# The last routing of a mixture-of-experts block: where the base table is built, in which order POOL lists and gathers, and which buffers the last products use

## The chip, the cores and the metric

The kernel runs on one core of one Trainium2 chip. TensorE (PE) multiplies and transposes, VectorE (DVE) and ScalarE (ACT) work elementwise, GpSimd (POOL) issues the indirect DMAs, SyncE (SP) issues the plain loads; ACT issues some plain DMAs too. The metric is device time in microseconds, lower is better.

## The reference, cut to what matters

There are 2048 tokens of 512 numbers, in float32. The first block is a layernorm, 16 heads of linear attention over 4 groups of keys, an output product with `Wo`, and the residual. The second block is a layernorm and a mixture of experts:

```python
scores = softmax(xf @ w_cls.T)                 # 64 logits: 32 experts, 32 that do nothing
_, topk_idx = top_k(scores + bias, 8)
w = take_along_axis(scores, topk_idx); w = w / (w.sum(-1) + EPS) * 1.5
# every expert takes its tokens in order, at most 256 of them
act = silu(x_e @ gate[e]) * (x_e @ up[e])      # 512 -> 256
y_e = act @ w_down[e]                          # 256 -> 512
out = (sum over a token's experts of w * y_e) * (1 + weights of the idle ones)
x = x + out
```

How many tokens an expert gets depends on the data, so the kernel finds at run time which rows each expert needs.

## The kernel before, in words

**The attention part.** Four blocks of 512 tokens run one after the other, each as four chunks of 128 tokens (16 chunks in all). `output` (L374 to L394) makes one chunk's output product `px` from 16 heads (L382; each shows as two matmuls in the trace), adds the residual into `x1` (L385), stores it (L386), takes mean and variance (L388, L390), lets POOL raise the variance to the power -1/2 (L263) and leaves the normalized chunk in `xw` (L393). A product of a chunk is 16 heads in order, and `between` lets other work in after the first 8.

**Routing.** `route` (L396 to L483) transposes `xw` (`prt`, L400), makes 64 logits (L405), finds the top 8 on DVE, writes the normalized row and its 32 weights to the array `rows` in HBM (L435), counts the position of each token within each expert, collects in `held` (L467) which token has which of the first 32 places of each expert, and leaves eight table addresses per token in `ai` (L482). `list_further` (L197) then issues eight indirect DMAs on POOL (`slots<-tok,ai`, L200). They write the token's number into eight tables in HBM. `place` has ranked the experts by their load of the first chunks, and places and tables go by that rank.

**Base and further places.** The first 32 places of each expert are the base. Four experts make one base group of 128 rows, so there are 8 groups. `rows_so_far` (L511 to L530) belongs to them: SP loads the tables' first 32 places (`idx_8b`, L516), DVE takes the lowest (`low`, L518; `low_f`, L520), PE transposes (`p_low`, L522), DVE spreads (`lowT`, L524), PE puts it in the experts' order (`p_place`, L526) and DVE reduces it to `idx_m_f` (L529, L530), the base table from the listings so far. It is called ahead of the product of the last chunk, chunk 15, and the routing of chunk 14 comes in the middle of that product. The last chunk's own part of the base comes from `held`; both meet in `idx_f` (L647 to L649) and `idx_b` (L650). The other places, 32 to 255, are read by ACT from the tables (`idx<-slots`, L835, eight loads), reduced by DVE (`idx_e`, L838), and put in order by PE and DVE (L840 to L847) into `idx`.

**The experts.** `gather` (L679) is an indirect DMA on POOL that fetches rows. `group_up` and `group_down` treat a base group: transposes (`pe_b`, L728), products (`pu_b`, L742), `act_b` (L746, L747), `aT_b` (L757), the down product, `y_b` (L762), a product that adds rows of the same token (`ps`, L764), `z` (L766) and a scatter-add of z into the output (L714). `over` treats one expert's further rows, 128 and 96: transposes (L728), `pu` (L786), `aT` (L789, L790), `py` (L801), a scaled `y` for the first part by ACT (L810) and for the second by DVE (L808), and a scatter-add of each (L714). The tiles `y` come from a pool of three buffers. The scatter-adds wait for one another one by one: y, y, z, y, y, z and so on. The first expert of each of the 8 groups always runs (two parts). The experts of rank 8 and up run in a nest of conditions, `further` (L868), which gathers ahead by three ranks (`xg_n`), and has a buffer `xg_r` for a second part. In the profiled run ranks 8, 9 and 10 ran, with one part each.

**Order.** Statements are put on the engines' queues by a planner that knows priorities and dependences; `issue_after` ties a statement's place to another's end in the queue. Each engine works its queue in order. Weights come in pairs of experts (`load_pair`, L185 and L194) on SP's queue, two of 1 MB and two of 0.5 MB a pair. The first three pairs are issued freely, and pair 3 waits for the second base gather (`behind`).

Of the kernel before, what the change touches and what calls it, by code (L numbers as in the profile page):

```python
# [9 lines left out]
F32 = mybir.dt.float32  # L10
# [3 lines left out]
ALU = mybir.AluOpType  # L14
# [4 lines left out]
P = 128  # L19
S = 2048  # L20
# [47 lines left out]
def linattn_moe(  # L68
# [125 lines left out]
            nc.sync.dma_start(out=dn[:, j], in_=wdn[bass.ds(v, 1)].rearrange("e (k p) f -> p (e k) f", p=P))  # L194
            weights[2 * i + j] = weights[2 * i + j], dn[:, j]

    def list_further(ch, ai):  # L197

        for k in range(TOPK):
            nc.gpsimd.indirect_dma_start(  # L200
                out=slots[k][:, :],
                out_offset=bass.IndirectOffsetOnAxis(ap=ai[:, k : k + 1], axis=0),
                in_=tok[:, ch : ch + 1],
                in_offset=None,
                bounds_check=NS - 1,
                oob_is_err=False,
            )


    with ExitStack() as ph:  # L210
# [163 lines left out]
        def output(sb, c, oTs, between=None):  # L374

            ch = sb * NC + c
            xs, _, _ = blocks[sb]
            px = p_pj.tile([P, D], F32, tag="pj", name=f"px_{ch}")
            for h in range(H):
                if between is not None and h == H // 2:  # L380
                    between()
                nc.tensor.matmul(px, lhsT=oTs[h // R][:, h % R, ts(c, P)], rhs=wo[h // R][:, h % R, :],  # L382
                                 start=(h == 0), stop=(h == H - 1))
            x1 = tmp.tile([P, D], F32, tag="row", name=f"x1_{ch}")
            nc.vector.tensor_tensor(x1, px, xs[:, c, :], ALU.add)  # L385
            tc.chain_iter_dep("out", nc.scalar.dma_start(out=out[ts(ch, P), :], in_=x1).ins)  # L386
            st = sml.tile([P, 6], F32, tag="st", name=f"st2_{ch}")
            nc.vector.bn_stats(st, x1)  # L388
            mv = sml.tile([P, 2], F32, tag="mv", name=f"mv2_{ch}")
            nc.vector.bn_aggr(mv, st)  # L390
            rstd = rstd_of(mv[:, 1:2], 1, f"2_{ch}")
            xw = tmp.tile([P, XW], F32, tag="xw", name=f"xw_{ch}")
            nc.vector.tensor_scalar(xw[:, :D], x1, mv[:, 0:1], rstd, ALU.subtract, ALU.mult)  # L393
            return xw  # L394
# [117 lines left out]
        def rows_so_far():  # L512

            idx_8b = tmp.tile([SL, TOPK, E], I32, tag="rb", name="idx_8b")
            for k in range(TOPK):
                nc.sync.dma_start(out=idx_8b[:, k, :], in_=slots_v[k][:SL, :E])  # L516
            low = sml.tile([SL, E], I32, tag="low", name="low", bufs=1)
            nc.vector.tensor_reduce(low, idx_8b.rearrange("s k e -> s e k"), AX.X, ALU.min)  # L518
            low_f = sml.tile([SL, E], F32, tag="hi", name="low_f")
            nc.vector.tensor_copy(low_f, low)  # L520
            pt = p_ms.tile([E, SL], F32, tag="ms", name="p_low")
            nc.tensor.transpose(pt, low_f, ident[:SL, :SL])  # L522
            lowT = sml.tile([E, Q, SL], F32, tag="fT", name="lowT", bufs=1)
            nc.vector.tensor_copy(lowT, pt.unsqueeze(1).to_broadcast([E, Q, SL]))  # L524
            pn = p_ms.tile([P, NQ, Q], F32, tag="ms", name="p_place")
            nc.tensor.matmul(pn, lhsT=lowT.rearrange("e j s -> e (j s)"), rhs=placed[:E, :E],  # L526
                             start=True, stop=True)
            part = sml.tile([P, NQ, Q], F32, tag="ad", name="part")
            nc.vector.tensor_tensor(part, pn, mine.unsqueeze(1).to_broadcast([P, NQ, Q]), ALU.mult)  # L529
            nc.vector.tensor_reduce(idx_m_f, part, AX.X, ALU.add)  # L530
# [15 lines left out]
        for sb in range(NSB):  # L546
            last = sb == NSB - 1
            if not last:
                blocks[sb + 1] = load_block(sb + 1)
            for g in range(G):  # L550
                if g == 0:
                    vas = [values(sb, c, xTs[sb]) for c in range(NC)]
                if g + 1 < G:
                    projs[sb, g + 1] = project(sb, g + 1, xTs[sb])
                elif not last:
                    xTs[sb + 1] = norm_block(sb + 1)
                    projs[sb + 1, 0] = project(sb + 1, 0, xTs[sb + 1])
                if last and g == 1:
                    rank_e = place()
                if last and g == G - 1:  # L560
                    for i in range(2):
                        load_pair(i)
                oT = otp.tile([P, R, SB], F32, tag="oT", name=f"oT_{sb}_{g}")
                oTs[sb, g] = oT
                for c in range(NC):
                    attend(sb, g, c, projs[sb, g], vas[c], oT)
                    if g == G - 1:
                        if c != 1 and waiting:
                            route_and_list(*waiting.pop(0))
                        if c >= 1:  # L570
                            waiting.append((sb * NC + c - 1,
                                            output(sb, c - 1, [oTs[sb, i] for i in range(G)])))
            listed = []
            if last:
                rows_so_far()
            xw = output(sb, NC - 1, [oTs[sb, i] for i in range(G)],
                        (lambda: listed.append(route(*waiting.pop(0)))) if last else None)
            with tc.issue_after(rstd_of.last.ins):
                for one in listed:
                    list_further(*one)  # L580
            while waiting:
                route_and_list(*waiting.pop(0))
            if last:
                route(sb * NC + NC - 1, xw)
            else:
                waiting.append((sb * NC + NC - 1, xw))
# [12 lines left out]
            nc.tensor.matmul(pn[:, i, :], lhsT=more_than[:, i : i + 1].to_broadcast([E, P]), rhs=of,  # L599
                             start=True, stop=True)  # L600
        big = sml.tile([P, 2, 2, E // 2], F32, tag="big", name="big")
        nc.vector.tensor_scalar(big.rearrange("p i a b -> p i (a b)"), pn, 0.5, None, ALU.is_ge)
        bigf = big.rearrange("p i a b -> p (i a) b")
        nc.vector.tensor_tensor(bigf, bigf, bits.unsqueeze(1).to_broadcast([P, 4, E // 2]), ALU.mult)
        bsum = sml.tile([P, 4], F32, tag="bsum", name="bsum")
# [11 lines left out]
    q_y = ctx.enter_context(tc.tile_pool(name="q_y", bufs=2, space=PSUM))  # L617
    NF = FI // P
    M2 = CAP - C2
    EARLY = 3  # L620
    FIRST = 2

    idx8 = xgp.tile([P, TOPK, 2 * E], I32, name="idx8")
# [15 lines left out]
    xg_b = [xgp.tile([P, XW], F32, name=f"xg_b{i}") for i in range(NQ)]  # L639
    xg_o = [xgp.tile([P, XW], F32, name=f"xg_o{i}") for i in range(2)]  # L640
    xg_t = [xgp.tile([P, XW], F32, name=f"xg_t{i}") for i in range(2)]
    xg_n = [xgp.tile([P, XW], F32, name=f"xg_n{i}") for i in range(3)]
    xg_r = xgp.tile([P, XW], F32, name="xg_r")
    for t in xg_o + xg_t + xg_n + [xg_r]:
        nc.scalar.mul(t, ident[:, 0:1].to_broadcast([P, XW]), 0.0)

    nc.vector.scalar_tensor_tensor(idx_f, held[:, :, 1], float(P), held[:, :, 0], ALU.mult, ALU.add)  # L647
    nc.vector.scalar_tensor_tensor(idx_f, idx_f, float(NONE), idx_m_f, ALU.add, ALU.min)
    nc.vector.tensor_tensor(idx_f, idx_f, nobody_f, ALU.min)  # L649
    nc.vector.tensor_copy(idx_b, idx_f)  # L650

    def find_same():

# [21 lines left out]
    def column(n, i):  # L675
        return idx[:, i * E + n : i * E + n + 1]

    def gather(t, i, n):
        return nc.gpsimd.indirect_dma_start(  # L679
            out=t,  # L680
            out_offset=None,
            in_=rows[:, :],
            in_offset=bass.IndirectOffsetOnAxis(ap=i, axis=0),
            bounds_check=n - 1,
            oob_is_err=False,
        )
# [85 lines left out]
    def over(e, parts, behind=None):  # L772
# [30 lines left out]
                at += k  # L803
        ys = []
        for i, (py, (xg, k)) in enumerate(zip(pys, parts)):
            y = yp.tile([P, D], F32, tag="y", name=f"y_{n}_{i}")
            if i:
                nc.vector.tensor_scalar(y[:k], py[:k], ws[i][:k], None, ALU.mult)  # L808
            else:
                nc.scalar.mul(y[:k], py[:k], ws[i][:k])  # L810
            ys.append((y[:k], column(e, i)[:k]))
# [5 lines left out]

    load_pair(2)
    base = []
    for q in range(EARLY):  # L820
        g = gather(xg_b[q], idx_b[:, q : q + 1], XR)
        base.append(g)
    for i in range(3, AHEAD_W):
        load_pair(i, base[1])
    with tc.issue_after(g.ins):
        list_further(S // P - 1, ai_last)
        for q in range(EARLY, NQ):
            gather(xg_b[q], idx_b[:, q : q + 1], XR)
    ahead = group_up(0)
# [19 lines left out]
    def gather_first(q):  # L849
        gather(xg_o[q % 2], column(Q * q, 0), S)  # L850
        return gather(xg_t[q % 2], column(Q * q, 1), S)

    def number_of(r):
        q, j = place_of(r)
        return Q * q + j

    def gather_rank(r):
        gather(xg_n[r % 3], column(number_of(r), 0), S)

    def reload(n, r):  # L860

# [8 lines left out]
    def further(r):  # L870

        n = number_of(r)
        with tc.If(more(0, r)):  # L873
            if n // Q < LATE:
                reload(n, r)
            with tc.If(more(1, r)) as cond:
                gather(xg_r, column(n, 1), S)
                over(n, [(xg_n[r % 3], P), (xg_r, M2)])
            with cond.Else():
                over(n, [(xg_n[r % 3], P)])  # L880
            if r + 3 < E:
                gather_rank(r + 3)
            if r + 1 < E:
                further(r + 1)

# [66 lines left out]
```

## Time and profile before

| what | value |
|---|---|
| median of the runs | 1140.47 us (three runs, 1138.63 to 1142.53) |
| the profiled execution | 1131.0 us, its span 1129.2 us, mean granted TensorE clock 0.964 |
| PE busy | 1025.8 us, 91% of the span |
| DVE, ACT, POOL busy | 607.5, 209.4, 229.8 us |
| scatter-adds into the output (L714) | 27, 19 of y and 8 of z, 2.6 / 5.8 / 8.5 us from issue to landing (min, median, max) |
| listing of the last chunk (`slots<-tok,ai_last`) | 8 DMAs, 2.6 / 5.1 / 6.3 us to landing |
| loads of the tables (`idx<-slots`) | 8 DMAs, 2.6 / 3.1 / 5.3 us to landing |
| base gathers (`xg_b<-rows,idx_b`) | 8 DMAs, median 3.8 us to landing |
| share of the 16 DMA engines in use | 0.38 at 880 to 900 us, 0.84 at 910 to 930, 1.02 at 950 to 1000, 0.26 at 1050 to 1080 |

A row of the timeline has the start in us, the duration in us, the engine (SPq, ACTq: a DMA issued by that engine's queue), the line, the operation, output and inputs by the program's names, shapes, and how many instructions were taken together; in brackets stands how long the engine had been idle and what ended that. A row of the waits has the waiting engine and line, what it waited for, and the total, the number and the longest of these waits. Figures after the share of the span are busy time; idle time of an engine that sets nothing costs nothing.

### The profile page before, as it was taken

What the parts mean: (1) busy time and instruction counts of PE and PEld (TensorE: products, weight loads), DVE (VectorE), ACT (ScalarE), POOL (GpSimd) and SP (SyncE); (2) the same over time, 40 slices, a digit from 0 to 9 for tenths busy, and PEclk for the clock granted to TensorE, in tenths of its full rate; (3) what the DMA queues carried; (4) which work ended last, traced back from release to release, by engine and by line L of the source; (5) the groups of instructions that cost most, each with busy time, mean ns of one, the idle gap of its engine ahead of it and who ended that gap; (6) DMA issues with size and microseconds to landing.
All of it is one profiled execution on the core that took longest, in us unless ns stands there. A gap on an engine that the chain in (4) does not pass through costs nothing. (4 is left out here: it accounts for less than half of the span.)

```text
span 1129.2 us, 12758 instructions
## 1 busy us (share of the span) xinstructions
PE 1025.8 (91%) x4420; PEld 581.3 (51%) x4420; DVE 607.5 (54%) x1661; ACT 209.4 (19%) x543; POOL 229.8 (20%) x290
## 2 busy tenths in 40 slices
PE   6999899999998999999899999999988677998883
PEld 3455455544655555455465544555643335675452
DVE  5778864347786733388847324778532532222220
ACT  1122221001233200122232001222200210111110
POOL 6000000431000044300001432000142364322332
PEclk9999999999999999999999999999999768999897
DMA  9400000010000000100000000023001379999220
GB/s 344 167 1 1 19 1 10 30 66 1 1 1 19 1 30 29 57 1 1 1 1 11 29 20 20 1 87 138 15 26 46 116 239 392 332 377 380 48 27 6
DMA packets 51805, 87.25 MB, mean 77 GB/s; under 512 B 11342, under 2 KB 11470, under 8 KB 51728
## 3 DMA queue, kind: packets, MB, share of 16 engines
q1 hardware_dynamic: 35248, 67.31, 16.2%
q0 software_dynamic: 10720, 10.08, 4.1%
q10 hardware_dynamic: 5760, 8.92, 2.1%
q8 instruction: 38, 0.62, 0.2%
q14 instruction: 39, 0.32, 0.1%
HBM read 75.92 MB, written 15.88 MB: 81 GB/s over the span
## 5 line engine op out<-in xcount | busy, mean ns | idle before, releaser
L382 PE MATMUL px<-wo,oT 128*128 128x512 f32 x512 | 234.7, 603 | 0.0
L324 PE MATMUL pq<-xT,wq 128*128 128x512 f32 x512 | 230.5, 595 | 0.5 <-DVE rb_q L306 0.4
L200 POOL DMA_INDIRECT slots<-tok,ai x120 | 117.7, 981 | 241.7 <-DVE ai L482 209.5
L324 PEld LDWEIGHTS pq<-xT,wq 128*128 128x128 f32 x512 | 93.5, 191 | 106.6 <-issue 91.7
L382 PEld LDWEIGHTS px<-wo,oT 128*128 128x128 f32 x512 | 94.5, 194 | 98.2 <-issue 98.1
L346 PE MATMUL po<-va,at 128*128 128x129 f32 x512 | 99.3, 280 | 12.1 <-DVE at L339 11.8
L355 ACT ACTIVATE osb<-po,den 128x128 f32<-128x128 f32 x256 | 77.7, 365 | 151.5 <-DVE den L353 85.6
L346 PEld LDWEIGHTS po<-va,at 128*128 128x128 f32 x512 | 80.0, 193 | 35.7 <-DVE at L339 23.3
L349 PE MATMUL po<-state,qT 128*128 128x129 f32 x480 | 93.6, 277 | 0.0
L295 POOL MEMSET va<- 128x4 f32 x16 | 1.5, 110 | 412.0 <-PE pst L362 412.0
L349 PEld LDWEIGHTS po<-state,qT 128*128 128x128 f32 x480 | 73.5, 193 | 1.3 <-DVE state L365 0.8
L371 PE MATMUL pot<-ident,osb 128*128 128x128 f32 x256 | 60.8, 302 | 14.5 <-ACT osb L355 13.3
L309 ACT ACTIVATE rb_q<-rb_q 128x512 f32<-128x512 f32 x64 | 40.3, 630 | 179.2 <-DVE rb_q L308 164.1
L385 DVE TENSOR_TENSOR x<-px,xs 128x512 f32<-128x512 f32 x16 | 11.1, 692 | 108.8 <-PE px L382 108.7
L371 PEld LDWEIGHTS pot<-ident,osb 128*128 128x128 f32 x256 | 36.1, 146 | 62.5 <-ACT osb L355 49.5
L337 PE MATMUL psc<-qT,kT 128*128 128x512 f32 x128 | 68.2, 616 | 0.0
L786 PE MATMUL pu<-xeT,gu 128*128 128x224 f32 (+1 forms) x352 | 63.8, 341 | 4.1 <-DVE xeT L729 4.1
L786 PEld LDWEIGHTS pu<-xeT,gu 128*128 128x128 f32 x352 | 60.3, 195 | 6.3 <-ACT y L810 2.3
L339 DVE TENSOR_TENSOR at<-psc,causal 128x512 f32<-128x512 f32 x64 | 44.0, 687 | 32.0 <-PE psc L337 31.9
L317 PE MATMUL pk<-xT,wk 128*128 128x512 f32 x128 | 58.9, 595 | 0.8 <-ACT xT L284 0.7
L372 DVE COPY oT<-pot 128x512 f32<-128x512 f32 x64 | 43.9, 686 | 25.8 <-PE pot L371 25.7
L292 PE MATMUL pv<-wv,xT 128*128 128x512 f32 x128 | 57.0, 596 | 0.0
(223 smaller groups left out, 1192.3 us busy)
## 6 DMA issues: line engine op xcount, KB each, us to landing
gu<-in_wgu_dram SPq DMA_DIRECT2D x32, 1024.0 KB, 12.0
dn<-in_wdn_dram SPq DMA_DIRECT2D x32, 512.0 KB, 12.4
rows<-xw ACTq DMA_DIRECT2D x16, 272.0 KB, 2.0
wq<-in_wqT_dram SPq DMA_DIRECT2D x4, 1024.0 KB, 14.8
wo<-in_woT_dram SPq DMA_DIRECT2D x4, 1024.0 KB, 14.6
out_dram<-x ACTq DMA_DIRECT2D x16, 256.0 KB, 2.1
xs<-in_x_dram SPq DMA_DIRECT2D x3, 1024.0 KB, 7.4
slots<-tok,ai POOLq DMA_INDIRECT x120, 2.1
```

The source lines that it names most:

```text
L200: nc.gpsimd.indirect_dma_start(out=slots[k][:, :], out_offset=bass.IndirectOffsetOnAxis(ap=ai[:, k : k + 1], axis=0), in_=tok[:, ch : ch + 1],
L292: nc.tensor.matmul(pvf, lhsT=xT[:, k, ts(c, P)], rhs=wv[:, k, :], start=(k == 0), stop=(k == KD - 1))
L317: nc.tensor.matmul(pk, lhsT=wk[:, k, ts(g, HD)], rhs=xT[:, k, :], start=(k == 0), stop=(k == KD - 1))
L324: nc.tensor.matmul(pq, lhsT=wq[g][:, k, ts(r, HD)], rhs=xT[:, k, :], start=(k == 0), stop=(k == KD - 1))
L337: nc.tensor.matmul(psc, lhsT=kT[:, cc], rhs=qT[:, :, cc], start=True, stop=True)
L339: nc.vector.tensor_tensor(at, psc, causal.unsqueeze(1).to_broadcast([P, R, P]), ALU.mult)
L346: nc.tensor.matmul(po[:, i, :], lhsT=at[:, r, :], rhs=va[:, g, :], start=True, stop=(old is None))
L349: nc.tensor.matmul(po[:, i, :], lhsT=qT[:, r, cc], rhs=old, start=False, stop=True)
L355: nc.scalar.mul(osb[:, 2 * j + i, :], po[:, i, :HD], den[:, i : i + 1])
L371: nc.tensor.transpose(pt[:, r, :], osb[:, r, :], ident)
L382: nc.tensor.matmul(px, lhsT=oTs[h // R][:, h % R, ts(c, P)], rhs=wo[h // R][:, h % R, :], start=(h == 0), stop=(h == H - 1))
L786: nc.tensor.matmul(pu[:, a, :m], lhsT=weights[e][0][:, k, a, c, :], rhs=xeT[:, k, :m], start=(k == 0), stop=(k == KD - 1))
```

## The change

The second half of `rows_so_far` becomes `rows_in_groups` and is placed behind the last output product's last matmul, ahead of the last routing. The last chunk's listing is split: three listings, then two base gathers (before: three gathers first), then the other five listings, then the other six gathers; `idx_b` is placed behind `big` no more but ahead of it in DVE's queue. The pool of `y` goes from three buffers to five. The ranked gathers keep two buffers of their own and take `xg_o[0]` and `xg_t[0]` as their third and fourth, and `xg_r` becomes `xg_o[1]`. In `further` the gather for three ranks on stands ahead of the expert's own product and scatter-add.

On the engines' queues this gives, in the built program:

- PE: the 16 heads' first half of the last product runs on into `prt` of chunk 14; `p_low` and `p_place` stand behind the last matmuls of chunk 14's routing (L464), ahead of `prt` of chunk 15. DVE: `lowT` ahead of the last `mv`, `part` ahead of the last `xw`, `idx_m_f` behind it. The loads of `idx_8b`, `low` and `low_f` stand where they stood, `low` between the last statistics of chunk 14 and its `xw`.
- POOL: listings 0 to 2, base gathers 0 and 1, listings 3 to 7, base gathers 2 to 7.
- ACT: the eight loads of the tables (L835) all stand ahead of the load of the activation table and the first `act_b`; before, one stood ahead and the others lay between the products' activations. DVE: `idx_e` stands between the two `act_b` of the first group, ahead of `same`, `later`, `dup` (L662 to L667), `y_b` and the second group's `xeT_b`; before, it stood behind all of these.
- SP: the same order; six of the weight loads (from pair 3 on) wait for a load of the tables each, since these share their semaphores.
- In the nest of conditions the last DMA of the kernel is a scatter-add; before, it was a gather whose rows nobody read.

```diff
-    def list_further(ch, ai):
+    def list_further(ch, ai, ks=range(TOPK)):
...
-        for k in range(TOPK):
-            nc.gpsimd.indirect_dma_start(
+        for k in ks:
+            one = nc.gpsimd.indirect_dma_start(
...
+        return one
...
-                nc.tensor.matmul(px, lhsT=oTs[h // R][:, h % R, ts(c, P)], rhs=wo[h // R][:, h % R, :],
-                                 start=(h == 0), stop=(h == H - 1))
+                output.last = nc.tensor.matmul(px, lhsT=oTs[h // R][:, h % R, ts(c, P)],
+                                                  rhs=wo[h // R][:, h % R, :],
+                                                  start=(h == 0), stop=(h == H - 1))
...
             nc.vector.tensor_copy(low_f, low)
+            return low_f
+
+        def rows_in_groups(low_f):
+
             pt = p_ms.tile([E, SL], F32, tag="ms", name="p_low")
...
             if last:
-                rows_so_far()
+                low_f = rows_so_far()
...
             if last:
+                with tc.issue_after(output.last.ins):
+                    rows_in_groups(low_f)
                 route(sb * NC + NC - 1, xw)
...
-    EARLY = 3
+    EARLY = 2
+    HEAD = 3
...
-    xg_n = [xgp.tile([P, XW], F32, name=f"xg_n{i}") for i in range(3)]
-    xg_r = xgp.tile([P, XW], F32, name="xg_r")
-    for t in xg_o + xg_t + xg_n + [xg_r]:
+    xg_n = [xgp.tile([P, XW], F32, name=f"xg_n{i}") for i in range(2)]
+    for t in xg_o + xg_t + xg_n:
...
-    nc.vector.tensor_copy(idx_b, idx_f)
+    listed = nc.vector.tensor_copy(idx_b, idx_f)
+    tc.add_manual_dep(flag.ins, listed.ins.name, ...
...
-            y = yp.tile([P, D], F32, tag="y", name=f"y_{n}_{i}")
+            y = yp.tile([P, D], F32, tag="y", name=f"y_{n}_{i}", bufs=5)
...
-    for q in range(EARLY):
-        g = gather(xg_b[q], idx_b[:, q : q + 1], XR)
-        base.append(g)
+    one = list_further(S // P - 1, ai_last, range(HEAD))
+    with tc.issue_after(one.ins):
+        for q in range(EARLY):
+            g = gather(xg_b[q], idx_b[:, q : q + 1], XR)
+            base.append(g)
     for i in range(3, AHEAD_W):
         load_pair(i, base[1])
     with tc.issue_after(g.ins):
-        list_further(S // P - 1, ai_last)
+        one = list_further(S // P - 1, ai_last, range(HEAD, TOPK))
+    with tc.issue_after(one.ins):
         for q in range(EARLY, NQ):
             gather(xg_b[q], idx_b[:, q : q + 1], XR)
...
+    xg_n += [xg_o[0], xg_t[0]]
+    xg_r = xg_o[1]
...
-        gather(xg_n[r % 3], column(number_of(r), 0), S)
+        gather(xg_n[r % 4], column(number_of(r), 0), S)
...
         with tc.If(more(0, r)):
+            if r + 3 < E:
+                gather_rank(r + 3)
...
-                over(n, [(xg_n[r % 3], P), (xg_r, M2)])
+                over(n, [(xg_n[r % 4], P), (xg_r, M2)])
...
-            if r + 3 < E:
-                gather_rank(r + 3)
             if r + 1 < E:
                 further(r + 1)
```

More of the change, by code (lines that the diff above doesn't have):

```diff
@@ L601, in linattn_moe @@
         big = sml.tile([P, 2, 2, E // 2], F32, tag="big", name="big")
-        nc.vector.tensor_scalar(big.rearrange("p i a b -> p i (a b)"), pn, 0.5, None, ALU.is_ge)
+        flag = nc.vector.tensor_scalar(big.rearrange("p i a b -> p i (a b)"), pn, 0.5, None, ALU.is_ge)
         bigf = big.rearrange("p i a b -> p (i a) b")
@@ L649, in linattn_moe @@
     nc.vector.tensor_tensor(idx_f, idx_f, nobody_f, ALU.min)
-    nc.vector.tensor_copy(idx_b, idx_f)
+    listed = nc.vector.tensor_copy(idx_b, idx_f)
+    tc.add_manual_dep(flag.ins, listed.ins.name,
+                      mybir.DependencyInfo(mybir.DependencyClass.NoSync, mybir.DependencyReason.DATA),
+                      reason="base rows come first")
     def find_same():
@@ L877, in further @@
                 gather(xg_r, column(n, 1), S)
-                over(n, [(xg_n[r % 3], P), (xg_r, M2)])
+                over(n, [(xg_n[r % 4], P), (xg_r, M2)])
             with cond.Else():
-                over(n, [(xg_n[r % 3], P)])
-            if r + 3 < E:
-                gather_rank(r + 3)
+                over(n, [(xg_n[r % 4], P)])
             if r + 1 < E:
```

## The prediction

> **What bounds the kernel now.** I read the page's slices first, then the timeline of the two stages that the change touches, then the waits and the chain that ended last.
>
> ```profile
> PEclk9999999999999999999999999999999768999897
> ```
>
> A slice is 28.2 us. PE is 91% busy, but in slices 31 to 33 (875 to 960 us), where the last routing hands over to the experts, its clock and its work sag. The timeline says why, first before chunk 15's product:
>
> ```profile
> 868.63 0.57 DVE L518 TENSOR_REDUCE low<-idx_8b 32x32 int32<-32x256 int32 x1 [4.94 <-DMA idx_8b<-slots]
> 869.45 0.20 PE L522 MATMUL p_low<-ident,low_f 32*32 32x32 f32 x1 [4.66 <-DVE low_f L520]
> 870.22 0.55 DVE L393 TENSOR_SCALAR xw<-x,mv,lnr 128x512 f32<-128x512 f32 x1 [0.75 <-POOL lnr L263]
> 872.10 3.78 PE L382 MATMUL px<-wo,oT 128*128 128x512 f32 x4
> 877.80 0.60 PE L400 MATMUL prt<-ident,xw 128*128 128x128 f32 x4
> 887.63 0.69 DVE L385 TENSOR_TENSOR x<-px,xs 128x512 f32<-128x512 f32 x1
> ```
>
> PE stands 4.66 us at p_low for the tables' landing, then works at half clock (windows 870 to 876: granted 0.50), four matmuls in 3.78 us. Then the hand-over:
>
> ```profile
> 905.34 1.06 POOL L679 DMA_INDIRECT xg_b<-rows,idx_b  x1 [4.74 <-issue]
> 918.33 0.97 POOL L200 DMA_INDIRECT slots<-tok,ai_last  x1 [0.30 <-issue]
> 919.69 0.27 ACT L757 COPY aT_b<-pa 128x128 f32<-128x128 f32 x1 [2.42 <-DMA slots<-tok,ai_last]
> 925.68 4.63 PE L742 MATMUL pu_b<-gu,xeT_b 128*32 128x256 f32 x64
> 928.44 1.07 DVE L838 TENSOR_REDUCE idx_e<-idx 128x64 int32<-128x512 int32 x1 [4.17 <-issue]
> 934.94 1.06 POOL L679 DMA_INDIRECT xg_o<-rows,idx  x1 [6.64 <-DVE idx L847]
> 941.24 1.11 PE L728 MATMUL pe<-ident,xg_o 128*128 128x128 f32 x4 [5.53 <-DMA xg_o<-rows,idx]
> ```
>
> The first expert starts at 941.24, after two base groups and the table of further places. From its scatter (956.71) the scatter-adds run one behind another, some 8.4 us apart while weights load (windows 950 to 1000: DMA share 1.02), some 4.8 after 1050. They lag ACT's y by up to 21 us, so this chain, not PE, sets the pace until the last expert:
>
> ```profile
> 1048.62 0.74 DVE L808 TENSOR_SCALAR y<-py,w 96x512 f32<-96x512 f32 x1 [9.52 <-DMA out_dram<-y,idx]
> 1050.02 2.08 PE L764 MATMUL ps<-y_b,same 128*128 128x512 f32 x2 [6.44 <-DVE y_b L762]
> 1106.46 1.57 POOL L714 DMA_INDIRECT out_dram<-y,idx  x1 [0.72 <-ACT y L810]
> 1113.14 1.56 POOL L714 DMA_INDIRECT out_dram<-y,idx  x1 [2.97 <-ACT y L810]
> 1115.83 1.08 POOL L679 DMA_INDIRECT xg_n<-rows,idx  x1 [1.13 <-PEq L873]
> ```
>
> ```profile
> DMA out_dram<-z,idx_s 4%; DMA out_dram<-y,idx 0%; POOL xg_n L679 0%; POOLq L873 0%; POOLq L679 0%; POOLq L714 0%
> ```
>
> The chain view's steps end in that scatter run and in a gather whose rows nobody reads.
>
> **The change, part by part.** The sum is made in the profiled execution (1131.0, span 1129.2), 9.5 us below the median 1140.47; I carry the difference over to the median.
>
> *Base table behind the product.* PE had done three heads (6 matmuls) by 864.79. Chunk 14's 26 matmuls took 11.40 us, 0.43 each, so the other five heads end at 869.1. Then prt waits for xw, which ends at 870.77. xw itself still stands behind `low`, since SP's loads stay. So prt starts near 870.8 instead of 877.80: 7.0 us. The wait is not gone, it is 1.7 instead of 4.66. The second half took 9.83 us (877.80 to 887.63) at a clock of 0.94, and the same is taken here. Moved work: lowT 0.27 and part 0.19 now stand in DVE ahead of chunk 15's xw, where nothing hides them: +0.4. p_low and p_place (0.2 and 0.6) lie in PE's wait of 2.99 before the last prt. Routing of chunk 15 thus ends 6.5 us earlier, `ai_last` at 896.0.
>
> That the clock stays up rests on two rows: 4.66 idle was followed by 0.50, 1.99 idle at 1024.9 by 1.00. If `low` came as late as the 4.66, some 10 matmuls at half clock would cost 4 us of the 7.0.
>
> *POOL's order.* A listing takes 1.29 a step, a gather 1.36. Three listings now stand ahead of the first gather and one gather less ahead of the fourth listing. Listings 0 to 2 run 896.3 to 900.1, gather 0 at about 900.3 (before 905.34: 5.0 earlier, not 6.5), listings 3 to 7 from 903.0 with the last at 908.2 (before 918.33: 10.1 earlier). Gathers 2 to 7 end near 917; their groups come much later. Dropping `idx_b` ahead of `big` is 0.7 that the listings cover. SP's pair 3 waits for gather 1: 905.3 instead of 910.4. Six loads behind it, in pairs 3 to 5, each wait for one table load; the last of them for the eighth, some 918, where that load now issued at 927.0. So they too are earlier, by 5 to 9 us.
>
> *ACT and DVE behind the tables.* This is the new wait. ACT's queue has all eight table loads ahead of the activation table's load (1.28) and both act_b. The eighth waits for listing 7's landing: 908.2 plus its end and 2.6 to 6.3 (median 5.1) gives 911 to 915, say 913.2. So act_b starts at about 915 (before 916.08), though pu_b is there 5 us sooner. `idx_e` on DVE waits for the eighth load's landing, 2.6 to 5.3 (median 3.1; the last one took over 5): 916 to 919, and it takes 1.07. Only then come the second act_b, same, later, dup (six, 0.7 each), y_b and xeT_b1. Before, these ran from 917.31. Behind them wait PE's pa, py_b, ps and pu_b1. With idx_e ending at 917 to 920, pu_b1 starts at 925 to 927 (before 925.68). From its start to the first xg_o gather were 9.26 us, PE-ordered (idx_ef was ready at 929.74, p_idx ran at 932.14), so the gather issues at 934.5 to 936.5, before 934.94. I take parity, +0.3; the ends are -4 (shortest landings, and PE's groups close up behind them) and +5 (longest landings). So the 6.5 and 10.1 us gained ahead are eaten here.
>
> *Loads 5 us sooner.* They leave a smaller backlog at 950 to 966, where the first two scatters were slow. A scatter is 8.4 us under loads and 4.8 without, so 5 us less of overlap is 5 x (1 - 4.8/8.4) = 2.1 us off the chain; bounds 0 (the loads' end stays near 1046, as buffers come free no sooner) and 5. I take 1.5.
>
> *Five y buffers.* DVE's two waits of 5.08 and 9.52 go, and with them PE's 1.99 and 6.44, 8.4 together. But each scatter-add still starts when the one before has landed, so the chain goes no faster. Only the last expert was bound by PE (1113.14, 2.97 behind ACT's y; the scatter ahead, at 1106.46, allows it at 1106.46 + 4.5 = 1110.96). That is worth 2.2 us; ends 0 and 8.4.
>
> The Trainium skill, "DMA: Bandwidth & Descriptors", "Rules for kernel authors", speaks against these buffers: an accumulating DMA must wait for the semaphore of an earlier one on the same bytes. The trace agrees: scatters wait 31.9 us for scatters. By that rule the buffers free PE and not the output; by the wait rows alone the sum would have 8.4 for the 2.2, in all -11.2.
>
> *Gather ahead of the last product.* The last DMA is now the scatter: it landed, by the 3.6 to 5.0 of late scatters, at about 1117.5; the unused gather at 1115.83 + 3.3 = 1119.1. That gives 1.6; ends 0 and 2. Buffers: gather 10 takes xg_o[0], free since about 1067, so no wait. ACT zeroes two buffers less, 1.3 us in its waits: nothing, as chunk 15's routing covered it.
>
> Sum: +0.3 - 1.5 - 2.2 - 1.6 = -5.0, so 1140.47 - 5.0 = 1135.5.
>
> **The rivals.** What a run can tell from no change is 0.3%, 3.4 us.
>
> 1. *Hidden anyway: the gain ends in the table wait and the chain.* The loads' end stays at 1046, so the 1.5 is 0; the first expert is 1.5 later, the last one's 2.2 is halved: 1.5 - 1.1 - 1.6 = -1.2, so 1139.3. For it: PE's 5.53 at the first expert and 2.42 on ACT are waits for landings, which moved work does not shorten. Chance 0.20.
> 2. *More: the early listing gets through.* The table lands at 914, idx_e ends at 915, pu_b1 at 921: the first expert is 4.5 earlier, the chain keeps it, and PE's 8.4 give 3: 4.5 + 2 + 3 + 1.6 = 11.1, so 1129.4. For it: base groups' weights lie ready, PE idles. Against: listing 7's landing in the same saturated stage (0.84). Chance 0.25.
> 3. *Slower: the first expert falls behind the tables.* The mechanism is the eight table loads on ACT ahead of act_b, and idx_e ahead of DVE's base work. If listing 7 takes 6.3 and its load 5.3 or more, now 5 us nearer to the weight loads' start, idx_e ends past 922, pu_b1 at 929 or later, and the chain starts 3.5 later. The point from which it decides: idx_e's end 5.3 us past my 919, 924, eats the whole 5.0. At 928 it gives +4: 1144.5. For it: six weight loads wait for table loads, and the engines' share was 1.05 at 914. Against: the listing itself is 10 us earlier. Chance 0.15.
>
> A rule speaks for the third: the Trainium skill, "Trainium Kernel Development and Optimization", "Key Constraints", says DMAs from SP, ACT and POOL run on the same 16 engines and interleave; the trace agrees, as scatters take 8.4 us beside loads and 4.8 without. It gives no price.
>
> **How the numbers follow.** The forecast has 0.40, 1135.5. Its own range is 1132 to 1139 (over(0) from -2 to +3). Below 1137 lie most of it and rival 2; faster by over 0.3% (under 1137.05) is 0.33 of the forecast's 0.40, all 0.25 of rival 2 and 0.04 of rival 1, together 0.62; within 0.3% are 0.07, 0.15 and 0.03 of rival 3, 0.25; slower (over 1143.9) is the rest of rival 3 and 0.01 of rival 1, 0.13. The range that leaves out 2 in 10 reaches into rivals 2 and 3: 1128 to 1144.
>
> **What will show it.** Right: prt of chunk 14 6 to 8 us before its old place relative to px14, no half clock from 870 to 876; listing 7 some 10 us and gather 0 some 5 us earlier; table loads all ahead of the first act_b on ACT, an act_b wait that ends on `slots<-tok,ai_last`, idx_e before `same`; the first pe of over within 2 us of 941 (relative to the seam's start); no DVE y wait of L808 for `out_dram`; scatter-adds still waiting for one another; the last DMA a scatter. Wrong: pe of the first expert before 937 (rival 2) or after 945 (rival 3), or scatters that no longer queue, so that PE's 8.4 us count in full.

## The result

On record are six runs of each kernel: 1133.59 us (1128.85 to 1135.13) against 1140.06 us before, a ratio on record of 0.992 with a 95% interval of 0.9899 to 0.9942 (the ratios of the record are estimates of their own; the two medians alone give 0.994, 6.5 us). The forecast was 1135.5, 5 us faster, so by this comparison it holds.

The experiments below put the two kernels side by side twice more, on other occasions. There the changed kernel took 1133.7 and 1133.2, as on record, but before took 1131.9 and 1131.5, and the ratios were 1.0011 (0.9987 to 1.0035) and 1.0018 (0.9997 to 1.0039). The time of the changed kernel is thus steady, and that of before was 8 to 9 us longer on the first occasion than on the three later ones (1130.8 is the third). None of those longer runs of before left a trace: its profiled execution took 1131.0, as the later ones. The three later occasions were on three chips (7, 9 and 3 on record); the chip of the first isn't on record. Where those 9 us lay stays open. The rest of this text explains the changed kernel's time by parts that repeat, and these say that the change as a whole is worth about nothing: one part gains 5 us, another loses as much or more.

### The profile after

The last part of the output product, by the timeline of the changed kernel. This execution runs 3.6 us behind that of before already at the routing of chunk 13 (`pp`, 856.55 instead of 852.95), ahead of everything that was changed, so places are compared by their distance from that.

```profile
872.24 0.57 DVE L520 TENSOR_REDUCE low<-idx_8b 32x32 int32<-32x256 int32 x1 [4.97 <-DMA idx_8b<-slots]
874.53 0.63 PE L402 MATMUL prt<-ident,xw 128*128 128x128 f32 x4 [1.85 <-DVE xw L395]
885.22 0.20 PE L528 MATMUL p_low<-ident,low_f 32*32 32x32 f32 x1 [0.68 <-DVE held L469]
887.59 0.66 PE L402 MATMUL prt<-ident,xw 128*128 128x128 f32 x4 [1.15 <-DVE xw L395]
```

PE waits 1.85 us instead of 4.66, for `xw`, as `low` still lands late (4.97 of waiting on DVE). The granted clock, by the windows of both kernels (us from and to; PE, PEld, DVE, ACT and POOL busy; PEclk; DMA share; GB/s; first the changed kernel):

```profile
871.00:876.00 5.00, 3.15 (x11) 1.18 (x10) 1.40 (x5) 0.59 (x1) 0.56 (x1) 1.00 0.62 216
```

```profile
870.00:876.00 6.00, 6.00 (x9) 2.37 (x9) 1.11 (x4) 0.00 (x0) 0.18 (x1) 0.50 0.49 168
```

In this stretch no half clock is left: 1.00 instead of 0.50. The last routing behind it runs at 0.50 in both kernels (894 to 899 us). The hand-over to the experts, from the timeline of the changed kernel's third trace (the run `after_again` below):

```profile
907.40 4.81 PE L753 MATMUL pu_b<-gu,xeT_b 128*32 128x256 f32 x48
913.04 3.00 ACTq L849 DMA_DIRECT2D idx<-slots  x3
916.21 1.28 ACT L757 ACT_TABLE_LOAD   x1 [25.59 <-DMA dn<-in_wdn_dram]
918.22 0.39 PE L766 MATMUL pa<-ident,act_b 128*128 128x128 f32 x1 [3.60 <-DVE act_b L758]
924.00 1.01 DVE L852 TENSOR_REDUCE idx_e<-idx 128x64 int32<-128x512 int32 x1 [5.84 <-DMA idx<-slots]
925.32 0.47 PE L766 MATMUL pa<-ident,act_b 128*128 128x128 f32 x1 [6.71 <-DVE act_b L758]
930.95 3.66 PE L753 MATMUL pu_b<-gu,xeT_b 128*32 128x256 f32 x64
939.24 1.06 POOL L690 DMA_INDIRECT xg_o<-rows,idx  x1 [5.67 <-DVE idx L861]
```

This is the new wait. ACT's load of the activation table stands behind its last table load, issued at 915.73, and that one waits for listing 7, issued at 909.80, to land 5.9 us later; the bracket names a weight load that landed at about that time. In the kernel before, ACT loaded the activation table as soon as PE was done with the first pu_b:

```profile
914.78 1.28 ACT L746 ACT_TABLE_LOAD   x1 [19.02 <-PE pu_b L742]
```

In the changed kernel DVE then stands 5.84 us at `idx_e` for the tables' landing, with the second act_b behind it, and PE stands 6.71 us at `pa` for that act_b. So the whole group is late, and the early listing does not come through.

The end of the changed kernel, from the timeline of its first trace:

```profile
1107.28 0.69 ACT L821 ACTIVATE y<-py,w 128x512 f32<-128x512 f32 x1 [1.54 <-PE py L812]
1113.89 1.56 POOL L725 DMA_INDIRECT out_dram<-y,idx  x1 [1.00 <-DMA out_dram<-y,idx]
1116.81 1.08 POOL L690 DMA_INDIRECT xg_n<-rows,idx  x1 [1.35 <-issue]
1118.19 1.57 POOL L725 DMA_INDIRECT out_dram<-y,idx  x1 [0.31 <-issue]
```

ACT's last y is ready 10 us ahead of its scatter-add; before, the scatter-add was issued 0.3 us behind it (1113.14, after 1112.18 + 0.69). So PE is out of the way and the run of scatter-adds alone sets the end. In the waits of the changed kernel DVE's y (now L819) waits for PE only, where it had waited 14.6 us for scatter-adds:

```profile
DVE y L819 <- PE py L812: 15.4, 8, 2.2
```

Every trace can be cut at the same three places: the routing of chunk 13 (`pp`), the first expert's first scatter-add and the last scatter-add. The four parts (start, hand-over, scatter-adds, tail) add up to the span but for rounding, in us:

| trace | start | hand-over | scatter-adds | tail | span |
|---|---|---|---|---|---|
| before (the profile shown first) | 853.0 | 103.8 | 156.4 | 16.1 | 1129.2 |
| before_look | 853.2 | 101.6 | 155.5 | 16.3 | 1126.5 |
| before_look2 | 854.8 | 101.6 | 154.0 | 16.2 | 1126.6 |
| before_again | 855.0 | 104.8 | 154.2 | 16.0 | 1129.9 |
| changed | 856.5 | 105.4 | 156.2 | 15.2 | 1133.4 |
| after_look | 856.2 | 105.4 | 159.5 | 15.2 | 1136.4 |
| after_again | 855.6 | 105.3 | 156.7 | 15.5 | 1133.1 |
| base_only | 856.4 | 97.6 | 156.9 | 16.3 | 1127.1 |
| pool_only | 856.2 | 111.9 | 155.7 | 16.0 | 1139.9 |
| y_cond | 851.9 | 101.8 | 152.9 | 15.2 | 1121.8 |
| base_y_cond | 857.5 | 95.6 | 155.9 | 15.4 | 1124.4 |
| base_y_cond_again | 856.1 | 99.2 | 155.8 | 15.5 | 1126.6 |
| late_tables | 855.2 | 98.6 | 153.4 | 15.3 | 1122.5 |
| held_loads | 852.9 | 104.3 | 152.1 | 15.2 | 1124.6 |

Against the four traces of before (means 854.0, 102.9, 155.0, 16.1) the changed kernel's three have +2.1 at the start, +2.5 in the hand-over, +2.5 in the scatter-adds and -0.8 in the tail. That overstates the loss: the three traced executions of the changed kernel took 1135.1, 1138.2 and 1134.8 us, all above its medians (1133.2 to 1133.7), and the four of before 1128.3 to 1131.7, at or under its later medians (1130.8 to 1131.9).

### The profile page after: what moved, and what is told of

It reads as the page before. It is cut to its first block, busy times and chain, and to the rows that moved or that the text cites. A ratio compares the mean times of both kernels' runs of the same rounds, so it can differ in the third digit from the quotient of the medians.

```text
span 1133.4 us, 12755 instructions
## 1 busy us (share of the span) xinstructions
PE 1025.8 (91%) x4420; PEld 583.2 (51%) x4420; DVE 607.0 (54%) x1661; ACT 208.5 (18%) x541; POOL 230.3 (20%) x290
## 3 DMA queue, kind: packets, MB, share of 16 engines
q1 hardware_dynamic: 35248, 67.31, 16.1%
## 4 chain that ended last, share of the span: by engine, by line
PE 55%; DVE 25%; issue 9%; DMA 5%; ACT 2%; POOL 1%; SPq 0%; ACTq 0%; POOLq 0%; DVEq 0%
PE px L383 16%; PE pq L325 5%; PE pu L797 4%; PE po L347 4%; PE psc L338 4%; DVE rb_q L306 3%; DVE rb_q L307 3%; DMA out_dram<-y,idx 3%; PE po L350 3%; PE pot L372 3%; DVE qT L308 3%; PE pv L293 3%; DVE qT L305 3%; DVE qT L311 3%; PE pk L318 2%
## 5 line engine op out<-in xcount | busy, mean ns | idle before, releaser
L383 PE MATMUL px<-wo,oT 128*128 128x512 f32 x512 | 231.7, 597 | 0.0
L356 ACT ACTIVATE osb<-po,den 128x128 f32<-128x128 f32 x256 | 77.8, 365 | 152.1 <-DVE den L354 99.4
```

What stands on the lines that cost most here:

```text
L356: nc.scalar.mul(osb[:, 2 * j + i, :], po[:, i, :HD], den[:, i : i + 1])
L383: output.last = nc.tensor.matmul(px, lhsT=oTs[h // R][:, h % R, ts(c, P)], rhs=wo[h // R][:, h % R, :], start=(h == 0), stop=(h == H - 1))
```

## The experiments

The theory that stood in the prediction (A): the base table's move shortens the hand-over by 6.5 us, and the waits for the tables on ACT and DVE, which POOL's order brings, take it back. Rivals: the scatter-adds hide all of it (B), or the base table's move is all that the change is worth (C).

**before_look: the unchanged kernel again.**

> The unchanged kernel again, for a second trace. In the profiled execution of the changed kernel PE is 3.6 us later than in that of before already at 853 to 857 us, ahead of anything that was changed, and PE stands eight times for about 1 us within the first pu_b with no cause shown (914 to 921). If the profiled execution of before (1131.0) was a quick one, this one is nearer to its median of 1140, and the extra 9 us lie at such places. If it again takes about 1131, the changed kernel's first expert (1.9 us later, once the 3.6 are taken off) is a true loss of the change.

It took 1128.27 (its span 1126.5), and the hand-over 101.6. So the profiled execution of before was no quick one. The hand-over of the changed kernel (105.3 to 105.4 in three traces) lies above all four of before (101.6 to 104.8). The 1 us gaps within the first pu_b (four of 1.0 to 1.5 us in the timeline, not eight) came in one of three traces of the changed kernel and are no part of the explanation.

**base_only: only the base table's move.**

```diff
-                rows_so_far()
+                low_f = rows_so_far()
...
+                with tc.issue_after(output.last.ins):
+                    rows_in_groups(low_f)
                 route(sb * NC + NC - 1, xw)
```

> Only the base table moved behind the output product; POOL, ACT and the y buffers as before. Theory A (the tables' waits eat the gain of the move): the queues of ACT and DVE are as before here, so nothing eats it and the run is 6 to 7 us faster than before, ratio 0.994. Theory B (the move is hidden behind the scatter-adds' chain in any case): within 1 us. Theory C (the move is all that the change is worth, and the other parts nothing): 6.5 us faster, and the other single parts within 1 us.

1124.21 against 1130.83: ratio 0.9955 (0.9934 to 0.9977), so 5.1 us faster by the ratio and 6.6 by the medians, with theory A's 6 to 7 within the interval. The hand-over is 97.6, 5.3 under the mean of before. B falls: what the hand-over gains does arrive at the end.

**pool_only: only POOL's order.**

```diff
-    EARLY = 3
+    EARLY = 2
+    HEAD = 3
...
+    one = list_further(S // P - 1, ai_last, range(HEAD))
...
+        one = list_further(S // P - 1, ai_last, range(HEAD, TOPK))
+    with tc.issue_after(one.ins):
         for q in range(EARLY, NQ):
             gather(xg_b[q], idx_b[:, q : q + 1], XR)
```

> Only POOL's order of listings and gathers and idx_b ahead of big, and with it the queues of ACT (all eight table loads ahead of the first act_b) and DVE (idx_e between the two act_b). Theory A: a loss of 3 to 8 us, since the first gather comes 1.4 us later and the base work stands for the tables; the first expert starts later by as much. Theory C: within 1 us. A third way, that the earlier listing reaches the first expert: 3.5 us faster.

The edit also places `idx_b` ahead of `big`, as the change does. 1141.3, ratio 1.0097 (1.0073 to 1.0122): 11 us slower, more than theory A gave, and C falls with it. The hand-over takes 111.9. Its timeline shows the same wait as the changed kernel, longer:

```profile
913.65 4.59 PE L747 MATMUL pu_b<-gu,xeT_b 128*32 128x256 f32 x64
922.84 1.28 ACT L751 ACT_TABLE_LOAD   x1 [25.49 <-DMA gu<-in_wgu_dram]
930.82 1.01 DVE L846 TENSOR_REDUCE idx_e<-idx 128x64 int32<-128x512 int32 x1 [6.02 <-DMA gu<-in_wgu_dram]
932.14 0.47 PE L760 MATMUL pa<-ident,act_b 128*128 128x128 f32 x1 [6.81 <-DVE act_b L752]
938.07 3.66 PE L747 MATMUL pu_b<-gu,xeT_b 128*32 128x256 f32 x64
```

PE is done with the first pu_b at 918.2. ACT can't take it until its table loads are issued, 4.6 us later; then `idx_e` holds the second act_b, and PE waits 6.81 us. Two brackets name weight loads, but `idx_e` started when the eighth table load landed (issued at 922.2, landed 8.5 us later, at 930.7).

**y_cond: only the y buffers and the ranked gathers.**

```diff
-            y = yp.tile([P, D], F32, tag="y", name=f"y_{n}_{i}")
+            y = yp.tile([P, D], F32, tag="y", name=f"y_{n}_{i}", bufs=5)
...
+            if r + 3 < E:
+                gather_rank(r + 3)
             if n // Q < LATE:
...
```

> Only the five y buffers, and the ranked gathers' buffers and order. Theory A: PE's 8.4 us of waits for y go, but the scatter-adds set the end: 2.2 us for the last expert and 1.6 us for the last gather, 3.8 us faster. If PE sets the end: 8 to 10 us faster. Theory C: within 1 us.

The ranked gathers' buffers are changed as well, as in the change. 1131.26, ratio 1.000 (0.9977 to 1.0022). PE's setting the end (8 to 10 us) is excluded, and so are the 3.8 us. Its one trace, at the quick end of its runs, has the scatter-adds 2.1 and the tail 0.9 under the means of before; the twelve runs (1123.6 to 1135.7) do not bear that out. In this kernel too the last y (1098.38 + 0.69) is ready 7.5 us ahead of its scatter (1106.59): freeing PE is worth what the scatter-adds let through, here at most 2.6 us.

**after_look: the changed kernel, beside the next two.**

> The changed kernel again, timed against before on the chip of the next three runs, with a second trace. The single parts gave, on one chip, 0.9955 (base table), 1.0097 (POOL's order) and 1.000 (y buffers and ranked gathers); if they add up the whole is 6 us slower than before there, ratio 1.005. Theory A as it stands now (the base table's move shortens the stage, POOL's order costs what ACT and DVE then wait for the tables, the y buffers free 2 to 3 us at the end): between 0.993 and 1.003, with ACT's load of the activation table later than the end of the first pu_b would allow, or pu_b itself late. The gaps of about 1 us within the first pu_b should be seen again if they belong to the change, and not if they belong to that one execution.

1133.7, ratio 1.0011 (0.9987 to 1.0035): within theory A's 0.993 to 1.003, while the 1.005 that the single parts would add up to lies outside the interval. The hand-over and its waits are those of the other two traces; the gaps in pu_b are not there.

**late_tables: the changed kernel, with seven table loads behind the first group's activations.**

```diff
...
+    first_acts = group_up.last
...
-    for k in range(TOPK):
-        nc.scalar.dma_start(out=idx8[:, k, :], in_=slots_v[k][SL:])
+    nc.scalar.dma_start(out=idx8[:, 0, :], in_=slots_v[0][SL:])
+    with tc.issue_after(first_acts.ins):
+        for k in range(1, TOPK):
+            nc.scalar.dma_start(out=idx8[:, k, :], in_=slots_v[k][SL:])
```

> The changed kernel with seven of ACT's eight table loads put behind the first group's activations on its queue, as before the change; idx_e then stands behind same, later, dup and y_b on DVE. Theory A: the new wait is gone, act_b starts when pu_b is done, the first expert is 5 to 9 us earlier than in the changed kernel, and the time is 4 to 8 us below it. Rival (the order of ACT's and DVE's queues does not matter, as the first expert waits for the tables' landing either way): within 2 us of the changed kernel.

1126.62, ratio 0.9962 (0.9944 to 0.9981), where the changed kernel had 1.0011 on the same occasion: some 7 us less by the medians, as theory A has it. The hand-over is 98.6 instead of 105.4, and the first expert's pe comes 83.0 us behind `pp` instead of 89.8. In the timeline the activation table is loaded as soon as PE is done, the second group's products start 12 us sooner than in the changed kernel (63.3 us behind `pp` instead of 75.3), and `idx_e` is no sooner than there (69.6 us, there 68.4 to 68.6):

```profile
912.17 1.28 ACT L757 ACT_TABLE_LOAD   x1 [19.88 <-PE pu_b L753]
918.45 1.46 PE L753 MATMUL pu_b<-gu,xeT_b 128*32 128x256 f32 x18
924.82 1.01 DVE L855 TENSOR_REDUCE idx_e<-idx 128x64 int32<-128x512 int32 x1 [5.27 <-DMA idx<-slots]
932.14 1.05 POOL L690 DMA_INDIRECT xg_o<-rows,idx  x1 [3.55 <-DVE idx L864]
```

The table is no sooner, yet the first expert is, because the base groups' work no longer queues behind it. The edit moves `idx_e` on DVE and the loads on ACT together, so the share of each wasn't told apart. With 1126.62 this kernel is level with base_y_cond, which has no part of POOL's order (1126.1, below, on the same occasion): once seven table loads are put back, no cost of POOL's order shows. One thing in this trace works against it: PE stood 1.96 us ahead of chunk 14's prt, where the changed kernel stood 1.82 to 1.85, the granted clock was 0.50 from 874 to 877 us, and `ai_last` was ready 2.2 us later (44.4 us behind `pp` instead of 42.2).

**base_y_cond: the change without POOL's order** (the edits of base_only and y_cond together).

> The change without POOL's order (and without idx_b ahead of big): the base table behind the product, five y buffers, ranked gathers as changed. Theory A: 5.1 us for the base table (0.9955 alone) and 2 to 3 for the last expert and the last gather: 7 to 8 us faster than before, ratio 0.993, and faster than the changed kernel. If POOL's order is what makes the change fast: slower than the changed kernel by 3 us or more.

1126.1, ratio 0.9948 (0.993 to 0.9967), on the same occasion as after_look and late_tables: 5.9 us faster than before, with theory A's 7 within the interval, and 7.6 us under the changed kernel by the medians.

**before_look2: the unchanged kernel, a trace from the same occasion.**

> The unchanged kernel, one more trace beside those of this call, so that places are compared on one chip: first expert (pe of over) near 939 to 941, last scatter-add near 1110 to 1113, span 1126 to 1130.

1128.31, span 1126.6; first expert at 940.3, last scatter-add at 1110.4.

**held_loads: why the tables land so late.** The weight loads of pairs 3 and 4 wait for the eighth table load; the queues of ACT and DVE stay as in the changed kernel.

```diff
...
-    for i in range(3, AHEAD_W):
-        load_pair(i, base[1])
...
+    for k in range(TOPK):
+        table = nc.scalar.dma_start(out=idx8[:, k, :], in_=slots_v[k][SL:])
+    for i in range(3, AHEAD_W):
+        load_pair(i, table)
     ahead = group_up(0)
...
-    for k in range(TOPK):
-        nc.scalar.dma_start(out=idx8[:, k, :], in_=slots_v[k][SL:])
```

> The changed kernel with the weight loads of pairs 3 and 4 held until the eighth table load has landed (the queues of ACT and DVE as changed). It asks why the last table loads land so late: in two traces of the changed kernel idx_e starts 32 us after the first table load is near (about 925.0), 8 to 9 us after the last table load is issued, where the trace of before had 2.6 to 5.3 us. If the weight loads beside them are the cause, idx_e starts 5 us or more earlier (before 920 with the first pp of chunk 14 at 856), and the first pu_b has no gaps of 1 us; the second pu_b then waits for its weights instead. If the tables land late for another reason (the listings themselves), idx_e stays near 925.

(The 32 us in that text is a slip: from the first table load, 901.2, to idx_e, 925.2, are 24.) The profile's timeline:

```profile
911.63 1.28 ACT L757 ACT_TABLE_LOAD   x1 [23.48 <-DMA idx<-slots]
914.07 1.01 DVE L852 TENSOR_REDUCE idx_e<-idx 128x64 int32<-128x512 int32 x1 [0.48 <-DMA idx<-slots]
915.39 0.47 PE L766 MATMUL pa<-ident,act_b 128*128 128x128 f32 x1 [1.42 <-DVE act_b L758]
923.16 1.05 PE L753 MATMUL pu_b<-gu,xeT_b 128*32 128x256 f32 x8 [1.65 <-DMA gu<-in_wgu_dram]
```

From `pp`, idx_e starts at 61.1 us instead of 68.4 to 68.6. The table loads' landing, from the view of that line, in held_loads and then in after_again (min, median, max, of seven and five of the eight loads, whose landing was recorded):

```profile
DMA to landing us min/median/max: 1.6/1.7/3.1
```

```profile
DMA to landing us min/median/max: 1.6/3.9/8.2
```

Listing 7 landed 3.8 us after its issue, where it took 5.9 in after_again. So the weight loads beside them make the tables late. As expected the second group then waits for its weights (`<-DMA gu`), and the hand-over, 104.3, is hardly shorter than the changed kernel's. Its one run took 1126.4, beside 1133.2 for the changed kernel on that occasion; the difference to the three traces lies in the start (2.7 to 3.6) and in the scatter-adds (4.1 to 7.4), and with one run it isn't settled.

**after_again, before_again, base_y_cond_again: the same three once more, side by side.**

> The changed kernel against before once more. It was 0.992 of before where before took 1140, and 1.001 (0.9987 to 1.0035) where before took 1132, itself 1133.6 and 1133.7. If its own time is steady and that of before differs by place, it is near 1134 again and the ratio follows before; if the gain of 6.5 us belongs to the change, the ratio is 0.992 again.

1133.24, ratio 1.0018 (0.9997 to 1.0039).

> The unchanged kernel timed against itself: what the comparison finds where nothing is changed. 1.000, within 0.0025 on either side.

1131.49 against 1131.54, ratio 0.9999 (0.998 to 1.0018): the comparison finds nothing where nothing is changed.

> The change without POOL's order once more, beside the changed kernel and before in one call: 0.9948 of before in the run ahead. Theory A: again 5 to 8 us under the changed kernel, whatever before takes. If POOL's order is what made the change fast where before took 1140: above the changed kernel.

1122.31, ratio 0.9919 (0.9894 to 0.9944), 10.9 us under the changed kernel, more than theory A's 5 to 8. Both times the change is better without POOL's order.

## Why the prediction was right, and where its steps were not

The forecast (1135.5, 5 us faster) agrees with the comparison on record and not with the two later ones, which find no gain: its range (1128 to 1144) holds the changed kernel's time in all three, its sign holds in the first alone. Most of its signs of being right hold as well: the first expert's pe, 942.7 in the frame of the prediction, lies within 2 us of 941. By its steps, each measured from `pp` as above:

- *Base table behind the product: 7.0 us at prt, 6.5 at the end of routing.* Measured: prt 18.0 us behind pp instead of 23.7 to 24.9, so 6.2 by the means; the last chunk's prt 31.0 instead of 36.7 to 37.8, so 6.1, and `ai_last` 6.1 too. The wait left was 1.85 where 1.7 was forecast, and the half clock is gone from this place. Alone this part gave 5.1 us. Right. That a wait of this length leaves the clock up holds in all but one of the traces with this move: in late_tables 1.96 us did not.
- *POOL's order: listing 7 10.1 us earlier, gather 0 5.0.* Measured 54.2 instead of 63.6 to 65.4 (9.9 us by the means), and 46.3 instead of 50.6 to 52.4 (4.8). Right as positions. As a price it was booked at nothing of its own, and it is the dear part: 11 us alone, and 8 to 11 us between the changed kernel and base_y_cond.
- *ACT and DVE behind the tables, taken at +0.3, ends -4 and +5.* The mechanism is right; its size is where the sum went wrong first. The step "the eighth load's landing, 2.6 to 5.3 (median 3.1...)" carried the landings of before over to a place beside 5 to 9 us earlier weight loads. The last of the eight took 7.7 and 8.2 us in the two traces that recorded landings; in the other, idx_e, which waited for it, started 9.1 us after its issue. So idx_e ended 69.5 us behind pp, which is 922.5 in the frame of the prediction, not 917 to 920, the second pu_b started 75.3 behind it (928.3, forecast 925 to 927), and the first expert's pe 89.8 instead of 87.1 by the means: +2.7 (+1.5 against the one trace that the prediction used). That lies within the ends, towards the third rival, which had named exactly this collision.
- *Loads sooner: -1.5.* Wrong, and in sign. Pair 3 was issued 51.5 to 51.6 us behind pp instead of 55.7 to 57.4, but the last weight load no sooner: 184.6 to 186.2, before 181.1 to 185.6. The first ten distances between scatter-adds from the first expert's on took 84.0 to 85.9 us, before 81.9 to 83.7, 2.8 more by the means. The first two took 9.4 and 9.6 us in the changed kernel's first trace (961.97, 971.41 and 980.96 by their issue), where before had 8.2 and 8.8. The overlap was not less at this place; what the sooner loads did was to delay the tables.
- *Five y buffers: -2.2.* The wait is gone as forecast, and scatter-adds set the end. At its place the gain is there: the last scatter-add follows the one ahead of it after 4.3 to 4.5 us, before after 4.9 to 6.7, 1.7 less by the means. In the time it didn't show: y_cond is 1.000, and the changed kernel's scatter-adds took 156.2 to 159.5 us in all, before 154.0 to 156.4.
- *Gather ahead: -1.6.* The tail is 15.2 to 15.5 instead of 16.0 to 16.3: -0.8. Right in sign, half in size.

So the positions ahead of the tables were right. Of the four terms of -5.0, the one for the tables had the mechanism right and the size too small (+0.3, measured +2.5 in the hand-over), the one for the loads had the wrong sign, and the two at the end were there in part (-1.7 and -0.8). The scatter-adds between, behind the first ten distances, took 1.4 us more by the means; no term was for them, and the cause stays open. Hand-over, scatter-adds and tail together give 2.5 + 2.5 - 0.8, 4 us slower by the traces; the medians of the two later comparisons are 1.7 and 1.8 us slower, and both intervals include 1.000. That the first comparison shows a gain of 6.5 us rests on the time of before there, which no trace explains. As far as the traces go, the agreement with the forecast is luck.

## What to carry to other kernels

When DMAs are issued earlier, look at what stands behind them in the queues of the engines that issue and read them: here a planner put eight table loads ahead of an activation, and one reduction ahead of an unrelated product's scaling. That order of POOL's work cost 11 us alone, and putting seven of the loads back gave 7 us. Small transfers that a stage waits for are not to be priced by their old landing times when large loads move beside them. And before a gain of under 1% is believed, time the unchanged kernel on another occasion too.

## What the runs showed of the hardware

- The same 32 KB table loads landed in at most 3.1 us where no weight load was issued beside them (held_loads, DMA share 0.23 to 0.32 from 897 to 911 us), and in up to 8.2 us with them, at a DMA share of 1.05 (910 to 925 us in after_again); in pool_only up to 8.5 us.
- The length of one wait of PE doesn't tell whether the clock goes down. Ahead of chunk 14's prt, waits of 1.81 to 1.85 us left it at 1.00 in seven traces, and 1.96 us in late_tables was followed by 0.50; 1.99 us at 1022.9 to 1024.9 in the trace of before left it at 1.00. In the changed kernel's first trace the clock was down from 888.6 us on, after waits of 0.68, 0.63, 1.15 and 0.73 us.
- PE stood four times for 1.0 to 1.5 us within one run of matmuls (914 to 921 in the changed kernel's first trace) with nothing that the profile shows to wait for. It was not there in two further traces of the same kernel:

```profile
915.67 0.42 PE L753 MATMUL pu_b<-gu,xeT_b 128*32 128x256 f32 x2 [1.01 <-issue]
917.12 0.39 PE L753 MATMUL pu_b<-gu,xeT_b 128*32 128x256 f32 x1 [1.02 <-issue]
```

- The start (up to `pp`) varied from 851.9 to 857.5 us among traces, and the runs of one kernel by 10 us and more (y_cond 1123.6 to 1135.7). Part of it is the granted clock in the attention part: from 340 to 353 us it was 1.00 in y_cond, 0.87 in before and 0.74 in after_again, and the stretch from the routing of chunk 2 to that of chunk 3 took 147.0, 148.7 and 149.3 us. Whether the place of a kernel's code or data has to do with it wasn't tried.
